# A graph layer on one core: where layernorm's transposition stands, who tests 37 of 50 rows, and how the last sum gets its operands

## The chip, the cores and the metric

The kernel runs on one core of one Trainium2 chip. Its time is the device time of one execution in microseconds; the number that counts is the median over the runs. One further execution was taken with the hardware profiler, and its trace is what the views below show.

The engines are called as in the profile: PE is TensorE (PEld its weight loads), DVE is VectorE, ACT is ScalarE, POOL is GpSimd, SP is SyncE, which only issues transfers here. Each engine works through its own instructions in order and waits where one of them needs something that another engine or a transfer has yet to finish.

## The reference

There are 6250 nodes with 128 channels (`x`) and 206,250 edges (`src`, `dst`), sorted by `dst`; a loop on each node is among them.

```python
h   = relu(layernorm(x))                      # per node, over the 128 channels
msg = concat(h[dst], h[src] - h[dst]) @ W.T + b
out = x + segment_max(msg, dst)               # maximum over the edges of each destination
```

As `W` has two halves, the message is `A[dst] + B[src]` with `A = h @ (W1 - W2).T + b` and `B = h @ W2.T`. `A` doesn't change within a segment. So `out = x + A + max over the edges of B[src]`.

## The kernel before, in words

Nodes are numbered `p * 49 + d`: partition `p` of 128 owns 49 destinations (`LD`), and its edges stand in a window of 1792 (`WIN`). Sources are numbered `q * 125 + l` (50 blocks `q`, 125 rows `l`). Most edges of a window are handled by one-hot matrices on PE; the rest, at most 440 to a partition after balancing (`KL`), are fetched row by row. The schedule is by hand: the order in which the Python code issues instructions is the order on each engine's queue (transfers on SP, ACT and POOL included).

**First stage (up to about 192 us).** `dst` and `src` windows are gathered. L736 turns `dst` into a float relative to the partition (`dlf`, on ACT), L740 makes `dl` of it, DVE makes `q16` of `src`, and then come 45 tests (`shift`, `deep`, `off`): DVE compares the keys with a shifted copy (`eq`, three buffers), PE adds the results in PSUM (`count`, `dup`). From this follow the edges that are alone in their cell and those that remain; `bases` (with a small product on PE, L606, whose result is `rowbase`), eleven `move`s and `spread` pack the remaining ones, POOL scatters them to `rest_list` in DRAM (L618, two scatters), and SP loads the balanced list from there (`qa<-rest_list`, L634). From that load DVE makes `ridx` (L808), the row numbers for the gathers.

Beside this runs layernorm with the products for A and B, in 30 calls of `step()`: six before the tests, three among them, three after them, and the rest in one go, all before `move` in the code. Call `i` works on five pairs of blocks at once. Before the change its order is:

```python
piece(i - 5, 1); piece(i - 4, 0); keep_all(i - 4); store(i - 4)  # ACT, and SP's stores of A and B
relu(i - 2)                                                      # ACT: pt -> hT
norm(i, 0); norm(i, 1)                                           # ACT: x -> xn
turn(i - 1)                                                      # PE: two transpositions xn -> pt
weigh(i - 3, 0); weigh(i - 3, 1)                                 # PE: hT times weights, and the bias
less(i - 4, 0)                                                   # PE: takes the rounded part of B away
```

In the profile `turn` is L667, `relu` L671, `weigh` L677 and L679, `less` L691, `piece` L687, `keep_all` L684, `norm` L662. `pt` is one tile with two halves. The stores go through SP's queue, ahead of the load of `rest_list`.

**Main loop (about 192 to 787 us).** There are 13 tiles of ten `l` values (the last of eight), 490 columns each, and 25 pairs of blocks to a tile: 325 turns `k`. In each, PE makes two products `z`, ACT turns them into one-hot columns (`oh`, L858), PE multiplies these with B in two pieces (`ps`, four matmuls, L943), and DVE takes the maximum (L947). Beside it the next tile is prepared: of the 50 rows of `OHQ`, row `a` up to `SQ` comes from ACT as a sign of `2 q - 2 a + 1` (`sgn`, L236, one instruction each), the others from DVE by comparison (`is_q`, L239), and PE takes the differences of neighbouring sign rows out again with the matrix `Diff`. DVE also makes `OHD` (L243, L246), and PE multiplies the two (L285).

The rest of the edges runs as a chain of rows: `gather_row` has POOL issue an indirect load of one row of B for each partition (L105, 440 of them), `stream_step` has DVE fold it into the row before (L188, `G`), and every eight rows SP writes them to `M`. A gather may be at most 16 rows ahead of the chain (`LEAD`). Gathers carry eight semaphores in turn, so each waits for the one eight before it. About 1.45 rows belong to a turn of the loop, 1.6 in the first tile. The chain is over at the first turn of the last tile, which the code calls `fixed` (`k` = 300).

**Last stage.** SP copies the last row to the next partition (`tail`, L956), DVE mends the heads with it, POOL scatters these to `M` (L960), and then POOL gathers the last row of each destination from `M` (`extract`, 49 gathers at L105), four at a time from `k` = 303 on. Meanwhile the last tile's turns run. At the end PE transposes the dense maxima, DVE takes the maximum with the extracted rows (L1002) and adds `xa` (L1007), and the result is stored in groups of eight. `xa` is A + x: at the first turn of the last tile SP loads A into it (L925), and at turn 15 of that tile POOL issues a load of `x` that adds to what is there (L899).

Of the kernel before, what the change touches and what calls it, by code (L numbers as in the profile page):

```python
# [31 lines left out]
F32 = mybir.dt.float32  # L32
# [6 lines left out]
AF = mybir.ActivationFunctionType  # L39
# [19 lines left out]
U = 8  # L59
# [1 line left out]
LEAD = 16  # L61
TL = 10
NEAR = 4
SQ = 25


def divisor_near(n, target, most):
# [3 lines left out]
def gnn_kernel(tc, x, src, dst, W, b, out):  # L71
# [42 lines left out]
    with ExitStack() as ctx:  # L114
# [13 lines left out]
        with ExitStack() as body:  # L128
# [81 lines left out]
            def onehots(t):  # L210

                if t >= len(tiles):
                    return [], []
                l0, nl = tiles[t]
                h = hots[t % 2]
                if t < 2:
                    oneh[t] = (h.tile([P, NBLK, Q + 1, TL], BF16, name="OHQ"),
                               h.tile([P, NBLK, WD, TL], BF16, name="OHD"))  # L220
                    G_.memset(oneh[t][0][:, :, 0], 1.0)
                else:
                    oneh[t] = oneh[t - 2]
                oq, od = oneh[t]
                ls = slice(l0, l0 + nl)

                def each(ap, b0, b1, n):

                    return at(ap, b0 * P + l0, [list(ap.ap[0]), [P, b1 - b0], [0, n], [1, nl]])

                def every(ap, b0, b1, n):

                    return at(ap, 0, [list(ap.ap[0]), [0, b1 - b0], [TL, n], [1, nl]])

                def sgn(a):
                    A_.activation(oq[:, :, a, :nl], TQ[:, :, ls], AF.Sign, scale=2.0, bias=sbias[:, a:a + 1])  # L236

                def is_q(b0, b1):
                    V.tensor_tensor(oq[:, b0:b1, SQ + 1:, :nl], each(TQ, b0, b1, Q - SQ), every(qq, b0, b1, Q - SQ),  # L239
                                    ALU.is_equal)  # L240

                def is_d():
                    V.tensor_tensor(od[:, :, :, :nl], each(TD, 0, NBLK, WD), every(jj, 0, NBLK, WD), ALU.is_equal)  # L243

                def val_of():
                    V.tensor_tensor(od[:, :, :, :nl], od[:, :, :, :nl], each(TV, 0, NBLK, WD), ALU.mult)  # L246

                def val_last():
                    def all_(ap):
                        return ap.rearrange("p (o b) -> p o b", o=1).to_broadcast([P, LD, NBLK])  # L250

                    od_last = oneh["last"] = accp.tile([P, LD, NBLK], BF16, name="od_last")
                    tdl = accp.tile([P, NBLK], BF16, name="tdl")
                    V.tensor_tensor(tdl, TD[:, :, P - 1], lob, ALU.subtract)
                    V.tensor_tensor(od_last, all_(tdl), dd.to_broadcast([P, LD, NBLK]), ALU.is_equal)
                    V.tensor_tensor(od_last, od_last, all_(TV[:, :, P - 1]), ALU.mult)

                half = NBLK // 2
                return [lambda a=a: sgn(a) for a in range(1, SQ + 1)], \
                       [lambda: is_q(0, half), lambda: is_q(half, NBLK), is_d, val_of] + \  # L260
                       [val_last] * (t == len(tiles) - 1)

            def products(t, bank):
# [42 lines left out]
            with ExitStack() as pre:  # L306
# [358 lines left out]
                def turn(i):  # L665
                    for j in range(2):
                        T_.transpose(st["pt", i][:, j, :L], st["xn", i][:, j], ident[:L, :L])  # L667
# [21 lines left out]
                def less(i, e):  # L689

                    T_.matmul(st["pm", i][:L, :, :C], negid[:L, :L], Bp[:L, e, 2 * i:2 * i + 2], start=False,  # L691
                              stop=True, skip_group_check=True)
# [11 lines left out]
                def step():  # L704


                    i = made["ln"]
                    made["ln"] = i + 1

                    def on(d):  # L710
                        return 0 <= i - d < NH

                    if on(5):
                        piece(i - 5, 1)
                    if on(4):
                        piece(i - 4, 0)
                        keep_all(i - 4)
                        store(i - 4)
                    if on(2):
                        relu(i - 2)  # L720
                    if on(0):
                        norm(i, 0)
                        norm(i, 1)
                    if on(1):
                        turn(i - 1)
                    if on(3):
                        weigh(i - 3, 0)
                        weigh(i - 3, 1)
                    if on(4):
                        less(i - 4, 0)  # L730

                STEPS = NH + 5
                for _ in range(6):
                    step()

                A_.activation(dlf, dwin, AF.Relu, bias=nthr)  # L736
                V.tensor_scalar(qa, swin, -62.0, 0.008, op0=ALU.add, op1=ALU.mult)
                V.tensor_scalar_add(qa, qa, MAGIC)
                V.tensor_scalar_add(q16, qa, -MAGIC)
# [15 lines left out]
                for n, f in enumerate(tests):  # L755
                    f()
                    if n == 6:
                        A_.activation(mids, mids, AF.Square)
                    if n % 14 == 8:
                        step()  # L760
                    elif n % 5 == 2 and early:
                        turned(*early.pop(0))
                    if n >= 20 and n % 5 == 0:
                        for g in signs[n - 20:n - 15]:
                            g()
                    if n in (12, 24, 36):
                        moments(3 + n // 12)
                        averages(3 + n // 12)
                        scales_a(3 + n // 12)
                    if n in (14, 26, 38):  # L770
                        scales_b(3 + n // 12)
                assert not early
                for g in signs[25:]:
                    g()
                cmp_.close()
                late = pre.enter_context(tc.tile_pool(name="late", bufs=1, side="right", reuse_waits="tile"))
                first = late.tile([P, W2], BF16, name="first")
# [25 lines left out]
                V.scalar_tensor_tensor(val, dlf, float(-L), first, op0=ALU.add, op1=ALU.mult)  # L803
                for b0 in range(0, NBLK, 4):
                    turned(val, TV, b0)
                for f in vals[:3]:
                    f()
                V.tensor_scalar(ridx, parts[:, 1:], 8191, None, op0=ALU.bitwise_and)  # L808
                vals[3]()
                bank0 = ps_m.tile([P, 512], F32, name="pm")  # L810
                mats, rest = products(0, lambda: bank0)
                for f in mats + rest:
# [26 lines left out]
            with ExitStack() as main:  # L839
# [51 lines left out]

                    return [flags, flagged] + [lambda a=a: find(a) for a in range(0, n8, 8)] + [rows_of_m]

                def add_x():

                    for p0, p1, g, n in ((0, P - 16, LD, 4), (P - 16, P - 1, LD, 4), (P - 1, P, LASTD, 2)):
                        m = g * C // n
                        assert m * n == g * C and m <= 2048
                        G_.dma_start(at(xa, 0, [[xa.ap[0][0], P], [m, n], [1, m]])[p0:p1],  # L899
                                     at(x, p0 * LD * C, [[LD * C, p1 - p0], [m, n], [1, m]]), accum_op=ALU.add, max_dma_last_dim=4 * m)  # L900

                oh = z_and_onehot(*pairs[0])
                soon, hot_fs = list(onehots(1)), [[], []]
# [2 lines left out]
                def due(k):  # L906

                    return min(NS, int(1.6 * min(k, NP_) + 1.45 * max(k - NP_, 0)))

                xa = None  # L910
                acc2 = None
                fixed, extracted, headed = 0, 0, False
                lasts = last_rows()
                for k, (t, i) in enumerate(pairs):
                    n = cols[t]
                    left = NP_ - i // 2
                    if i == 0:
                        acc2 = two.tile([P, 2, 512], F32, name="acc2")
                        if t == len(tiles) - 1:
                            hotx.close()  # L920
                            fin = main.enter_context(tc.tile_pool(name="fin", bufs=3, side="right",
                                                                  reuse_waits="tile"))
                            xa = fin.tile([P, LD, C], F32, name="xa", bufs=1)
                            for p0, p1, d0, g in ((0, P - 16, 0, LD), (P - 16, P - 1, 0, LD), (P - 1, P, 0, LASTD)):
                                nc.sync.dma_start(xa[p0:p1, d0:d0 + g], at(At, p0 * LD * C, [[LD * C, p1 - p0], [1, g * C]]))  # L925

                            nc.sync.dma_start(xa[P - 1:P, LASTD:], at(At, 0, [[LD * C, 1], [1, (LD - LASTD) * C]]))
                        new_products = products(t + 1, lambda: ps_v.tile([P, 512], F32, name="pv"))
                        mats, rest = new_products or ([], [])
                        if t:  # L930
                            hot_fs = list(onehots(t + 2))
# [31 lines left out]
                    elif fixed and k > fixed + 2 and k % 2:  # L963
# [2 lines left out]
                            if d == extracted:  # L966
                                follow(g, maxed)
                        extracted = min(extracted + 4, LD)
                    if xa is not None and i == 30:
                        add_x()  # L970
                    some(soon[0], 10 - i // 2)
                    some(soon[1], 8 - i // 2)
                    some(hot_fs[0], left - 5)
# [7 lines left out]
                                          for j in range(2)), ALU.max)  # L981
                    if k % 6 == 0 and k > 2 * NP_ and lasts:
                        lasts.pop(0)()
                assert state["ran"] == NS and fixed + 2 < len(pairs)
                for d in range(extracted, LD):
                    extract(d)
                mid.close()
# [5 lines left out]
                acc_v = acc.rearrange("c (p d) -> c d p", d=LD)  # L993
                for d0 in range(0, LD, U):
                    g = min(U, LD - d0)
                    o = fin.tile([P, U, C], F32, name="o", bufs=3)
                    for j0 in range(0, g, 4):
                        j1 = min(j0 + 4, g)
                        pf = ps_f.tile([P, 4, P], F32, name="pf")
# [77 lines left out]
```

## Time and profile before

| | |
|---|---|
| median of 3 runs | 888.58 us (886.48 to 889.82) |
| profiled execution, own time | 884.34 us |
| its span | 882.5 us |
| busy PE, DVE | 707.6 us, 707.5 us (80% each) |
| busy ACT, POOL | 527.8 us, 524.6 us (60%, 59%) |
| first gather of B's rows starts | 192.35 us |
| last one starts | 772.23 us |
| first and last extraction gather start | 797.00 us, 871.65 us |

Busy shares are means over the three stages, which have different limits; each stage has to be read by itself. In a row of the timeline the first number is the start in us, the second the time until the last of the merged instructions ended; behind the shapes stands in brackets how long the engine had been idle, and who ended that. In the waits, the numbers are total us, times and the longest. A group's row gives busy us, mean ns of one, and the idle time ahead of them with what ended it.

### The profile page before, as it was taken

To read this page: it belongs to the slowest core of one execution; us is meant where nothing else is said; L and a number is where in the kernel's file an instruction comes from. 1 tells how busy PE (TensorE), PEld (TensorE's weight loads), DVE (VectorE), ACT (ScalarE), POOL (GpSimd) and SP (SyncE) were. 2 spreads that over 40 slices of the span, in tenths; PEclk is the share of its full clock that TensorE was granted. 3 is DMA by queue.
4 is the path that set the end of the run, shared out by engine and by line. 5 is a ranking of instruction groups with operands and counts; after the bars stand their busy time and mean duration, and the time that the engine had idled before them with its cause. 6 is when DMAs were issued, how large, how long until landed. Compare 5 with 4: busy or idle time off the path is not lost. (4 is left out here: it accounts for less than half of the span.)

```text
span 882.5 us, 13139 instructions
## 1 busy us (share of the span) xinstructions
PE 707.6 (80%) x4275; PEld 501.4 (57%) x4275; DVE 707.5 (80%) x1177; ACT 527.8 (60%) x1224; POOL 524.6 (59%) x582
## 2 busy tenths in 40 slices
PE   1478776767999999999999999999898989849310
PEld 0234343454767776767676666667666767538210
DVE  6499779537899999999998889989898998737223
ACT  0424644437787878787778677777777776626000
POOL 4500000127777777777777777777777777707734
PEclk9999855557999999999999999999999999968655
DMA  6550022221454333333333333333333333451384
GB/s 155 148 117 24 24 64 53 59 78 48 150 194 141 123 97 123 100 99 96 99 97 113 103 103 99 100 100 98 99 96 101 103 112 108 140 138 47 76 184 135
DMA packets 48467, 91.39 MB, mean 104 GB/s; under 512 B 10964, under 2 KB 30395, under 8 KB 48036
## 3 DMA queue, kind: packets, MB, share of 16 engines
q0 software_dynamic: 17264, 40.98, 18.6%
q1 hardware_dynamic: 30120, 49.04, 16.6%
q10 hardware_dynamic: 1009, 0.49, 0.3%
q8 instruction: 34, 0.56, 0.3%
q14 instruction: 40, 0.33, 0.1%
HBM read 45.64 MB, written 44.71 MB: 102 GB/s over the span
## 5 line engine op out<-in xcount | busy, mean ns | idle before, releaser
L105 POOL DMA_INDIRECT G<-Bt,ridx x440 | 445.6, 1013 | 163.8 <-issue 88.1
L858 ACT ACTIVATE oh<-z 126x490 fp32r<-126x490 f32 (+1 forms) x650 | 335.5, 572 | 165.7 <-PE z L857 164.3
L943 PE MATMUL ps<-oh,Bp 126*128 126x490 f32 (+1 forms) x1300 | 395.6, 427 | 36.4 <-DVE acc L947 31.0
L947 DVE TENSOR_TENSOR acc<-acc,ps 128x980 f32<-128x980 f32 (+1 forms) x312 | 360.0, 1154 | 12.6 <-PE ps L943 10.4
L943 PEld LDWEIGHTS ps<-oh,Bp 126*128 126x128 f32 x1300 | 242.3, 195 | 126.3 <-DVE acc L947 70.0
L857 PE MATMUL z<-Vf,Sel 114*126 114x490 f16 (+1 forms) x650 | 198.1, 384 | 10.1 <-ACT oh L858 7.9
L188 DVE SCALAR_TENSOR_TENSOR G<-G,slim 128x128 f32<-128x128 f32 x439 | 152.9, 348 | 48.6 <-DMA G<-Bt,ridx 43.0
L236 ACT ACTIVATE OHQ<-TQ,sbias 128x140 bf16<-128x140 bf16 (+1 forms) x325 | 122.7, 413 | 0.5
L285 PEld LDWEIGHTS <-OHQ 128*51 128x51 bf16 x1792 | 92.1, 184 | 39.7 <-issue 39.7
L857 PEld LDWEIGHTS <-Sel 114*126 114x126 f16 x650 | 81.9, 139 | 30.6 <-issue 3.6
L285 PE MATMUL pv<-OHD,OHQ 128*51 128x13 bf16 (+5 forms) x1638 | 94.9, 240 | 0.5 <-ACT OHQ L236 0.5
L618 POOL DMA_INDIRECT rest_list<-qa,base_i x2 | 3.4, 1706 | 110.4 <-DVE qa L627 108.2
L105 POOL DMA_INDIRECT G<-M,last_e x48 | 45.5, 948 | 27.6 <-issue 14.5
L667 PE MATMUL pt<-ident,xn 125*128 125x125 f32 x50 | 16.1, 419 | 41.9 <-ACT hT L671 32.4
L554 PE MATMUL dup<-eq,identb 128*128 128x512 bf16 (+1 forms) x180 | 40.7, 361 | 9.3 <-DVE eq L559 7.9
L687 ACT CAST Bp<-pm 125x256 fp32r<-125x256 f32 x50 | 16.2, 374 | 50.8 <-PE pm L691 48.6
L677 PE MATMUL pm<-wT,hT 128*125 128x256 f32 x100 | 43.3, 582 | 0.0
L1001 PE MATMUL pf<-ident,acc 128*128 128x128 f32 x49 | 10.6, 391 | 34.5 <-DVE o L1002 32.8
L667 PEld LDWEIGHTS pt<-ident,xn 125*128 125x128 f32 x50 | 7.0, 193 | 49.5 <-ACT hT L671 39.3
L554 PEld LDWEIGHTS <-identb 128*128 128x128 bf16 x180 | 17.5, 99 | 29.2 <-issue 14.5
L1007 DVE TENSOR_TENSOR o<-o,xa 128x1024 f32<-128x1024 f32 (+1 forms) x7 | 7.7, 1093 | 31.4 <-DMA xa<-in_x 31.2
L677 PEld LDWEIGHTS pm<-wT,hT 128*125 128x125 f32 x100 | 27.5, 303 | 4.0
(236 smaller groups left out, 472.5 us busy)
## 6 DMA issues: line engine op xcount, KB each, us to landing
M<-G SPq DMA_DIRECT2D x63, 512.0 KB
G<-Bt,ridx POOLq DMA_INDIRECT x440, 2.6
xa<-At SPq DMA_DIRECT2D x1, 2744.0 KB
xa<-in_x POOLq DMA_DIRECT2D x1, 2744.0 KB
G<-in_x SPq DMA_DIRECT2D x6, 448.0 KB
Bt<-ba SPq DMA_DIRECT2D x12, 224.0 KB
At<-ba SPq DMA_DIRECT2D x12, 224.0 KB
out_x<-o SPq DMA_DIRECT2D x3, 512.0 KB
```

Of the source, the lines that this page charges most:

```text
L105: return G_.indirect_dma_start(out=o, out_offset=None, in_=table, in_offset=bass.IndirectOffsetOnAxis(ap=idx, axis=0))
L188: steps.append(V.scalar_tensor_tensor(G[:, j], state["prev"], slim[:, k:k + 1], G[:, j], op0=ALU.min, op1=ALU.max))
L236: A_.activation(oq[:, :, a, :nl], TQ[:, :, ls], AF.Sign, scale=2.0, bias=sbias[:, a:a + 1])
L285: T_.matmul(o, oq[:, b_, :, l], r, start=k == 0 and b_ == 0, stop=b_ == NBLK - 1, skip_group_check=True)
L554: T_.matmul(dup[:, c0:c1], identb, e[:, c0:c1], start=s == 1, stop=s == SH + 2)
L667: T_.transpose(st["pt", i][:, j, :L], st["xn", i][:, j], ident[:L, :L])
L677: T_.matmul(pm[:L, j], st["hT", i][:, j, :L], wT, start=j == 0, stop=False, skip_group_check=True)
L687: A_.copy(Bp[:L, e, 2 * i:2 * i + 2], st["pm", i][:L, :, :C])
L857: T_.matmul(z[:, :n], Sel[:, i + j], Vf[t % 2][:, :n], start=True, stop=True)
L858: A_.activation(oh[:, j, :n], z[:, :n], AF.Relu)
L943: T_.matmul(ps[:, j, :n], Bp[:, e, i + j], oh[:, j, :n], start=e == 0, stop=e == 1)
L947: maxed = V.tensor_tensor(acc2[:, :, :n], acc2[:, :, :n], ps[:, :, :n], ALU.max)
```

## The change

Four things are changed.

- `turn(i - 1)` moves from the middle of `step()` to its end, behind `weigh` and `less`.
- `SQ` goes from 25 to 37: ACT makes 37 rows of `OHQ` by signs, and DVE compares 13 (before 25). DVE's comparison comes as one instruction instead of two. The first tile's signs are spread over the tests in groups of three.
- The conversion of `dst` goes from ACT to DVE.
- `xa` is filled differently. A and x come in four pieces of 13, 13, 13 and 10 destinations to a partition, both loaded by SP (x into a tile `xo` of its own with two buffers), at the 3rd, 7th, 11th and 15th turn after `fixed`; DVE adds the first two pieces at the 11th and 15th turn, the others between the groups of output. POOL's adding load is gone. The output tile `o` has two buffers instead of three.

```diff
-SQ = 25
+SQ = 37
...
-                return ... [lambda: is_q(0, half), lambda: is_q(half, NBLK), is_d, val_of] + \
+                return ... [lambda: is_q(0, NBLK), is_d, val_of] + \
...
                     if on(0):
                         norm(i, 0)
                         norm(i, 1)
-                    if on(1):
-                        turn(i - 1)
                     if on(3):
                         weigh(i - 3, 0)
                         weigh(i - 3, 1)
                     if on(4):
                         less(i - 4, 0)
+                    if on(1):
+                        turn(i - 1)
...
-                A_.activation(dlf, dwin, AF.Relu, bias=nthr)
+                V.tensor_scalar(dlf, dwin, nthr, 0.0, op0=ALU.add, op1=ALU.max)
...
-                    if n >= 20 and n % 5 == 0:
-                        for g in signs[n - 20:n - 15]:
-                            g()
+                    if n >= 18 and n % 2 == 0:
+                        for g in signs[:3]:
+                            signs.pop(0)()
...
-                def add_x():
-                    for p0, p1, g, n in ((0, P - 16, LD, 4), (P - 16, P - 1, LD, 4), (P - 1, P, LASTD, 2)):
-                        ...
-                        G_.dma_start(<xa[p0:p1]>, <x>, accum_op=ALU.add, max_dma_last_dim=4 * m)
+                def load_some():
+                    d0 = adds[-1][1] if adds else 0
+                    d1 = min(d0 + XG, LD)                    # XG = 13
+                    xo = fin.tile([P, XG, C], F32, name="xo", bufs=2)
+                    for o, ap in ((xa[:, d0:d1], At), (xo[:, :d1 - d0], x)):
+                        ...                                  # nc.sync.dma_start for 112, 15 and 1 partitions
+                    adds.append((d0, d1, xo))
+                def add_some(n):
+                    d0, d1, xo = adds[n]
+                    V.tensor_add(xa[:, d0:d1], xa[:, d0:d1], xo[:, :d1 - d0])
...
                             xa = fin.tile([P, LD, C], F32, name="xa", bufs=1)
-                            for p0, p1, d0, g in ...:
-                                nc.sync.dma_start(xa[p0:p1, d0:d0 + g], <At>)
...
-                    if xa is not None and i == 30:
-                        add_x()
+                    if fixed and k - fixed in (11, 15):
+                        add_some((k - fixed) // 4 - 2)
+                    if fixed and k - fixed in (3, 7, 11, 15):
+                        load_some()
...
                 for d0 in range(0, LD, U):
-                    o = fin.tile([P, U, C], F32, name="o", bufs=3)
+                    if d0 in (16, 32):
+                        add_some(1 + d0 // 16)
+                    o = fin.tile([P, U, C], F32, name="o", bufs=2)
```

More of the change, by code (lines that the diff above doesn't have):

```diff
@@ L256, in val_last @@
                     V.tensor_tensor(od_last, od_last, all_(TV[:, :, P - 1]), ALU.mult)
-                half = NBLK // 2
                 return [lambda a=a: sgn(a) for a in range(1, SQ + 1)], \
-                       [lambda: is_q(0, half), lambda: is_q(half, NBLK), is_d, val_of] + \
+                       [lambda: is_q(0, NBLK), is_d, val_of] + \
                        [val_last] * (t == len(tiles) - 1)
@@ L771, in gnn_kernel @@
                         scales_b(3 + n // 12)
-                assert not early
-                for g in signs[25:]:
-                    g()
+                assert not early and not signs
                 cmp_.close()
@@ L805, in gnn_kernel @@
                     turned(val, TV, b0)
-                for f in vals[:3]:
+                for f in vals[:2]:
                     f()
                 V.tensor_scalar(ridx, parts[:, 1:], 8191, None, op0=ALU.bitwise_and)
-                vals[3]()
+                vals[2]()
                 bank0 = ps_m.tile([P, 512], F32, name="pm")
@@ L892, in last_rows @@
                     return [flags, flagged] + [lambda a=a: find(a) for a in range(0, n8, 8)] + [rows_of_m]
-                def add_x():
-                    for p0, p1, g, n in ((0, P - 16, LD, 4), (P - 16, P - 1, LD, 4), (P - 1, P, LASTD, 2)):
[L897 to L900, printed above, removed]
+                def load_some():
[3 more added lines that the diff above has]
+                    for o, ap in ((xa[:, d0:d1], At), (xo[:, :d1 - d0], x)):
+                        for p0, p1, g in ((0, P - 16, d1), (P - 16, P - 1, d1), (P - 1, P, min(d1, LASTD))):
+                            if g > d0:
+                                nc.sync.dma_start(o[p0:p1, :g - d0],
+                                                  at(ap, (p0 * LD + d0) * C, [[LD * C, p1 - p0], [1, (g - d0) * C]]))
+                        g = max(d0, LASTD)
+                        if d1 > g:
+                            nc.sync.dma_start(o[P - 1:P, g - d0:], at(ap, 0, [[LD * C, 1], [1, (d1 - g) * C]]))
+                    adds.append((d0, d1, xo))
+                def add_some(n):
+                    d0, d1, xo = adds[n]
+                    V.tensor_add(xa[:, d0:d1], xa[:, d0:d1], xo[:, :d1 - d0])
                 oh = z_and_onehot(*pairs[0])
@@ L908, in due @@
                     return min(NS, int(1.6 * min(k, NP_) + 1.45 * max(k - NP_, 0)))
+                XG = 13
+                adds = []
                 xa = None
@@ L923, in gnn_kernel @@
                             xa = fin.tile([P, LD, C], F32, name="xa", bufs=1)
-                            for p0, p1, d0, g in ((0, P - 16, 0, LD), (P - 16, P - 1, 0, LD), (P - 1, P, 0, LASTD)):
-                                nc.sync.dma_start(xa[p0:p1, d0:d0 + g], at(At, p0 * LD * C, [[LD * C, p1 - p0], [1, g * C]]))
-                            nc.sync.dma_start(xa[P - 1:P, LASTD:], at(At, 0, [[LD * C, 1], [1, (LD - LASTD) * C]]))
                         new_products = products(t + 1, lambda: ps_v.tile([P, 512], F32, name="pv"))
@@ L983, in gnn_kernel @@
                         lasts.pop(0)()
-                assert state["ran"] == NS and fixed + 2 < len(pairs)
+                assert state["ran"] == NS and tiles[-1][0] == pairs[fixed][0] * TL and adds[-1][1] == LD
                 for d in range(extracted, LD):
```

## The prediction

> **What bounds the kernel now.** I read the page first, then windows over the stages, the waits, the timeline of one layernorm step, and the timeline of the last hundred microseconds. Three stages have three different limits.
>
> The windows, columns being busy us of PE, PEld, DVE, ACT, POOL, then granted clock, DMA share and GB/s:
>
> ```profile
> 100.00:130.00 30.00, 18.58 (x50) 11.24 (x50) 22.64 (x23) 15.60 (x42) 0.00 (x0) 0.57 0.20 51
> 130.00:160.00 30.00, 20.73 (x52) 12.50 (x53) 29.10 (x33) 13.92 (x39) 1.35 (x2) 0.50 0.22 60
> 160.00:192.00 32.00, 21.25 (x65) 12.99 (x64) 7.00 (x7) 13.85 (x37) 2.06 (x1) 0.55 0.30 80
> ...
> 495.00:542.00 47.00, 43.79 (x277) 30.91 (x277) 42.02 (x66) 34.31 (x77) 36.03 (x37) 1.00 0.33 105
> ```
>
> From 100 to 192 us no engine is full and PE has half its clock: a chain is running. The waits say which:
>
> ```profile
> DVE o L1007 <- DMA xa<-in_x: 31.2, 1, 31.2
> ...
> POOL G L105 <- DVE ridx L808: 30.3, 1, 30.3
> DVE ridx L808 <- DMA qa<-rest_list: 25.0, 1, 25.0
> ...
> DVE dl L740 <- ACT dwin L736: 11.0, 1, 11.0
> ```
>
> The first gather (192.35) waits for `ridx`, that for the load of `rest_list`, and this load stands on SP behind every layernorm store, though its scatters were issued by 162. So layernorm's pace ends last. One step takes 4.80 us (130.19 to the next `turn` at 135.00), in single file:
>
> ```profile
> 129.73 0.41 ACT L671 ACTIVATE hT<-pt 128x250 f32<-128x250 f32 x1
> ...
> 130.19 0.68 PE L667 MATMUL pt<-ident,xn 125*128 125x125 f32 x2 [1.51 <-ACT hT L671]
> ...
> 130.66 1.92 PE L677 MATMUL pm<-wT,hT 128*125 128x256 f32 x4
> ...
> 132.51 0.47 PE L679 MATMUL pm<-b,onesb 3*125 3x256 bf16 x1
> ...
> 132.91 0.58 PE L691 MATMUL pm<-Bp,negid 125*125 125x256 f32 x1
> ...
> 133.52 0.65 ACT L687 CAST Bp<-pm 125x256 fp32r<-125x256 f32 x2 [2.64 <-PE pm L691]
> ```
>
> PE's `turn` stands first in its queue and waits for ACT's `relu`; ACT stands still for 2.64 us until `less` ends.
>
> In the main loop the page's costliest group tells it:
>
> ```profile
> L105 POOL DMA_INDIRECT G<-Bt,ridx x440 | 445.6, 1013 | 163.8 <-issue 88.1
> ```
>
> Without the 30.3 us ahead of the first, 133.5 us of idle lie before 439 gathers: 0.304 us each, an issue gap. POOL never waits longer, so it sets the pace: 1.013 + 0.304 = 1.317 us a row, 36.25 rows a tile, 47.7 us; the tiles take 47. DVE, PE and ACT have slack.
>
> At the end:
>
> ```profile
> 766.52 1.49 SPq L925 DMA_DIRECT2D xa<-At  x3
> ...
> 771.80 0.35 DVE L188 SCALAR_TENSOR_TENSOR G<-G,slim 128x128 f32<-128x128 f32 x1 [2.97 <-DMA G<-Bt,ridx]
> ...
> 777.10 0.35 DVE L188 SCALAR_TENSOR_TENSOR G<-G,slim 128x128 f32<-128x128 f32 x1 [3.86 <-DMA G<-Bt,ridx]
> ...
> 840.38 0.94 POOL L105 DMA_INDIRECT G<-M,last_e  x1 [0.30 <-issue]
> 850.91 0.94 POOL L105 DMA_INDIRECT G<-M,last_e  x1 [9.59 <-DMA xa<-in_x]
> ```
>
> The 3.1 MB load of `xa` starves the last six gathers, so the chain of rows ends at 786.6 though the last was issued at 772.2; later POOL's own adding load blocks its extraction gathers.
>
> **The change part by part**, in time of the profiled execution: span 882.5, own time 884.34, which is 4.24 under the median of 888.58.
>
> *DVE converts dst.* DVE idled 10.97 us before L740 (41.57). The conversion costs it about 1.2 us (L737, the same size from int32: 1.218), and its tests could start at 36 instead of 45.7. PE comes later: it must finish six layernorm steps, 42.46 before. With `turn` last in them I work them to 39.7 (each `weigh` starts one ACT relay earlier). Three `eq` buffers let DVE run ahead, then its fourth test waits for the first count, 1.3 us at slow clock: 41.0 against 48.69. Gain 7.7 us.
>
> *`turn` last.* New order on PE: `weigh` 1.85, bias 0.40, `less` 0.42, `turn` 0.47, the start-to-start times above: 3.14 us. ACT's `pieces`, `keep_all`, `relu`, `norm` take 2.2 us (133.52 to 135.7) and now run during `weigh`. So a step costs 3.14 at the slow clock. At full clock (91.09 to 92.8) PE needs 1.70, and ACT's 2.2 would be the limit. First use: L606 came after three such steps, `rowbase` at 114.53; now DVE's own `heads` (109.15 - 7.7 = 101.5) ends last and `rowbase` comes at 102.3: 12.2 earlier. DVE then runs unbroken to the scatters (156.39 and 159.95 become 144.2 and 147.8), landed by about 152, as the second waited 3.56 for the first. Second use: fourteen whole steps from 102.2 end at 133 (2.2) or 146 (3.14), the four lighter ones and stores add 6 to 10: SP is free at 139 to 156. What is late next is therefore the scatters or, at slow clock, the stores. `rest_list` takes 2.58 (188.61 to 191.19): `ridx` at 154.6 to 158.3 instead of 191.19. I take 156: **35 us gained**. The clock rows weigh both ways: 0.50 to 0.57 in this stage with PE 62 to 69% busy, 1.00 in the main loop at 93%; the new step would be full. [...]
>
> *37 rows by signs.* DVE's two `is_q` of 1.067 become one of about 1.10 (L243, the same 1820 elements): 1.03 us less per tile, which DVE's slack hides. It touches POOL, though: at 501.01 a gather took 1.74 where `is_q` began at 500.86, 1.76 at 509.38 beside `is_d`. 35 of the 440 gathers took over 1.1 us, 19.9 us in excess of 0.95; four such DVE operations per tile become three, so a quarter goes: **5 us gained** (0 to 9). ACT gets twelve signs more per tile at 0.30 to 0.415: 3.6 to 5.0 us on 34.3 of 47; covered. (The first tile's fall among the tests, where ACT is busy 16.65 of 30 us.) If the cover went, see the third rival. In the first tile four signs stand beside a pair instead of three (1.2 + 0.92 = 2.1 us a pair against the 2.1 of 1.6 rows): 0 to 3 us; I take 0, because POOL is then up to 16 rows ahead.
>
> *Load of xa moved.* It now stands on SP behind the last `M<-G` and `tail<-G`, so the last gathers land undisturbed: a gather landed 2.42 after its start in the chain (812.02), then two DVE rows of 0.3: the chain of rows ends 3.0 after the last gather instead of 14.4: **11.4 gained**.
>
> *From the end of the rows to the end.* Before: 10.4 until the first extraction (`tail` 6.3, `head`, scatter), 74.65 from the first to the 49th, 10.85 to the end; 95.9. Now the three loads on POOL (3.2 us), their 11.9 of waits and more leave: 48 x 1.245 = 59.8. Against it stand 6.27 MB of loads beside the gathers, some 26 us at 240 GB/s (3.74 MB in 15.5 us from 766.5). Under such a load a gather landed only every 2.85 us (771.80 to 785.89, five intervals). With eight in flight (each waits for the one eight before) I count 16 issued where 18.5 would have been: 3 us lost, and 1.6 on `head`'s scatter. Bounds: nothing, or 20 if everything waits until the loads are through. 12.0 + 59.8 + 3 + 10.85 = 85.7: **10.2 gained**. DVE's four adds of 1664 elements cost 2.0 each (1.227 per 1024), and two stand between the last tile's pairs: a late piece stalls PE there, but these pairs need 27 us and POOL 60, so it is hidden. Fewer `o` buffers: groups come every 10 us, hidden. [...]
>
> Sum: 35 + 5 + 11.4 + 10.2 = 61.6. Own time 884.3 - 61.6 = 822.7; on the runs' median 888.6 - 61.6 = **827**.
>
> **Rivals.**
> 1. Layernorm's relay stays: `turn` and `relu` still take turns at 4.8 us. Then only the 7.7 of the conversion is gained in front, 34.3 in all: 854. For it: ACT's `relu` still waits for `turn`. Against: `weigh`, the longest piece, no longer stands behind that.
> 2. The loads choke the extraction: `head`'s scatter waits for the first two pieces, and gathers land at 2.85 throughout, 15 to 20 instead of 4.6 us: 840. For it: the rows at 771 to 786. Against: pieces three and four wait for DVE's adds.
> 3. Slower: ACT becomes the main loop's bound. It decides where a pair's chain, `z` 0.58, relus 1.05 and two signs 0.82, runs in series: 2.45 against 1.88 us in 17 pairs of 12 tiles, 116 us: 943. From 2.18 us a pair on it eats the whole gain. Against: the first tile has three signs a pair already, and its relus start at 212.35, 214.17, 216.00, 1.83 apart.
>
> **How the numbers follow.** Forecast 0.68, first rival 0.12, second 0.14, third 0.06. Range: the good ends together (clock 1.4, signs 4, no contention 4.6, and profiles against medians up to 4) give 813, a little below it 808; the bad ends (layernorm 2.3, signs 5 and 3, tail 15) give 852, with the first rival 855. Faster by over 0.5% (4.4 us, about what a measurement can tell from no change): 0.93; within: 0.01; slower: 0.06.
>
> **What would show it.** First gather at 156 to 160; a `turn` every 2.2 to 3.2 us; gather mean near 1.00 us with gaps still 0.30; no wait of DVE `G` for its gather over 1 us at the end; the first extraction 12 us after the last row, POOL unbroken afterwards. A wait of POOL on DVE in the main loop, or of ACT's `relu` as long as 2.6 us, would make it wrong.

## The result, and the profile after

| | before | after |
|---|---|---|
| median | 888.27 us (886.48 to 889.82, 4 runs) | 828.64 us (827.97 to 830.31, 4 runs) |
| profiled execution, own time | 884.34 us | 829.12 us |
| its span | 882.5 us | 827.4 us |

The ratio is 0.9332, with an interval of 0.9309 to 0.9355: 59.6 us are gained on the medians. The forecast was 827. Between the two profiled executions only 55.1 us lie, because the profiled run of before was 3.9 under its median and that of after 0.5 above its own. The prediction's sum was 61.6, made against the profile. So the forecast came closer than its sum did, and the sum is what has to be examined.

**First stage.** The first lines are from the timeline of after (start, duration, engine, line; idle time ahead in brackets): two successive layernorm steps, from one `turn` (L666) to the next.

```profile
111.36 0.43 PE L666 MATMUL pt<-ident,xn 125*128 125x125 f32 x2
111.62 1.03 PE L676 MATMUL pm<-wT,hT 128*125 128x256 f32 x4
...
112.58 0.32 PE L678 MATMUL pm<-b,onesb 3*125 3x256 bf16 x1
...
112.90 0.46 ACT L670 ACTIVATE hT<-pt 128x250 f32<-128x250 f32 x1
113.13 0.38 PE L690 MATMUL pm<-Bp,negid 125*125 125x256 f32 x1 [0.23 <-ACT ba L683]
...
113.42 0.43 PE L666 MATMUL pt<-ident,xn 125*128 125x125 f32 x2
```

A step takes 2.06 us instead of 4.80. PE goes from `turn` straight into `weigh`, and `relu` starts when PE's bias product ends and runs beside `less`. The window over 90 to 136 us (busy us of PE, PEld, DVE, ACT, POOL, then granted clock, DMA share, GB/s), of before and then of after:

```profile
90.00:136.00 46.00, 32.20 (x112) 18.87 (x112) 36.92 (x41) 24.28 (x66) 0.00 (x0) 0.66 0.17 45
```
```profile
90.00:136.00 46.00, 38.25 (x157) 23.99 (x154) 41.74 (x35) 40.73 (x113) 0.00 (x0) 0.93 0.43 112
```

PE issues 157 instead of 112 instructions and gets a clock of 0.93 instead of 0.66; `weigh` falls from 582 to 435 ns. ACT, busy 40.73 of 46, now sets the step: PE waits 0.23 us for it ahead of each `less` (DVE's 41.74 are the packing). How much of the shorter step is the order itself and how much the clock is not shown, as no run holds the clock down. Behind that, the timeline shows what ends last:

```profile
135.67 0.83 SPq L698 DMA_DIRECT2D At<-ba  x2
...
143.00 1.30 POOL L617 DMA_INDIRECT rest_list<-qa,base_i  x1 [91.69 <-DVE qa L626]
...
146.56 2.10 POOL L617 DMA_INDIRECT rest_list<-qa,base_i  x1 [2.26 <-DVE first L798]
150.28 0.35 SPq L633 DMA_DIRECT2D qa<-rest_list  x1
152.78 0.39 DVE L805 TENSOR_SCALAR ridx<-qa 128x440 int32<-128x440 int32 x1 [0.90 <-DMA qa<-rest_list]
153.95 1.12 POOL L105 DMA_INDIRECT G<-Bt,ridx  x1 [5.29 <-DVE ridx L805]
```

SP issues its last layernorm store at 135.67, before the scatters. These now end last, and `ridx` waits 0.90 us for its load instead of 25.0.

**Main loop.** The page's group and the waits:

```profile
L105 POOL DMA_INDIRECT G<-Bt,ridx x440 | 443.0, 1007 | 138.9 <-issue 89.3
```
```profile
POOL G L105 <- issue: 102.4, 337, 0.3
```

A gather takes 1007 instead of 1013 ns, with the same 0.30 us behind it. The first to the last gather take 577.36 us (153.95 to 731.31) against 579.88.

**The end.** From the timeline:

```profile
733.93 0.35 DVE L188 SCALAR_TENSOR_TENSOR G<-G,slim 128x128 f32<-128x128 f32 x1 [0.35 <-DMA G<-Bt,ridx]
...
735.59 3.10 SPq L899 DMA_DIRECT2D xa<-At  x3
...
742.18 1.00 POOL L967 DMA_INDIRECT M<-head,head_i  x1 [9.93 <-DVE head L966]
...
751.80 0.97 POOL L105 DMA_INDIRECT G<-M,last_e  x1 [8.62 <-DVE acc L954]
...
753.60 1.89 DVE L909 TENSOR_TENSOR xa<-xa,xo 128x1664 f32<-128x1664 f32 x1
...
754.34 1.96 POOL L105 DMA_INDIRECT G<-M,last_e  x1 [0.30 <-issue]
```

The chain of rows ends at 734.28, 3.0 after the last gather. But the first extraction starts 9.62 us after `head`'s scatter, where before it started 3.00 after it:

```profile
794.00 1.00 POOL L960 DMA_INDIRECT M<-head,head_i  x1 [20.83 <-DVE head L959]
797.00 0.97 POOL L105 DMA_INDIRECT G<-M,last_e  x1 [2.00 <-issue]
```

The wait is put down to a maximum of DVE; the first extraction follows the one of its own turn, which had long been done, so the scatter's landing was the suspect. A second thing to see is the gather of 1.96 us beside DVE's add.

### The profile page after: what moved, and what is told of

It reads as the page before. It is cut to its first block, busy times and chain, and to the rows that moved or that the text cites. A ratio compares the mean times of both kernels' runs of the same rounds, so it can differ in the third digit from the quotient of the medians.

```text
span 827.4 us, 13330 instructions
## 1 busy us (share of the span) xinstructions
PE 678.8 (82%) x4270; PEld 488.1 (59%) x4275; DVE 704.5 (85%) x1169; ACT 566.7 (68%) x1379; POOL 523.5 (63%) x579
## 4 chain that ended last, share of the span: by engine, by line
DVE 24%; PE 23%; DMA 19%; issue 14%; ACT 11%; POOL 8%; SPq 1%; POOLq 0%; ACTq 0%; DVEq 0%
DMA G<-Bt,ridx 13%; PE ps L950 10%; DVE acc L954 9%; POOL G L105 8%; PE z L854 5%; ACT oh L855 5%; PE pv L284 4%; ACT OHQ L236 3%; DVE G L188 3%; DVE dwin L598 3%; DVE eq L558 2%; DVE qa L597 1%; PE dup L553 1%; DMA w_sb<-in_L_gnn_W 1%; DMA xo<-in_x 1%
## 5 line engine op out<-in xcount | busy, mean ns | idle before, releaser
L105 POOL DMA_INDIRECT G<-Bt,ridx x440 | 443.0, 1007 | 138.9 <-issue 89.3
L236 ACT ACTIVATE OHQ<-TQ,sbias 128x140 bf16<-128x140 bf16 (+1 forms) x481 | 170.1, 414 | 0.5
L105 POOL DMA_INDIRECT G<-M,last_e x48 | 50.2, 1046 | 22.9 <-issue 13.1
L1013 DVE TENSOR_TENSOR o<-G,pf 128x512 f32<-128x512 f32 x12 | 8.1, 685 | 29.5 <-DMA G<-M,last_e 28.3
L553 PEld LDWEIGHTS <-identb 128*128 128x128 bf16 x180 | 17.7, 99 | 25.8 <-issue 11.4
L676 PE MATMUL pm<-wT,hT 128*125 128x256 f32 x100 | 30.6, 435 | 0.3 <-DVE rowbase L606 0.3
L558 DVE TENSOR_TENSOR eq<-KA,KB 128x1792 bf16<-128x1792 int16 x22 | 23.9, 1088 | 0.8 <-PE dup L553 0.8
L1012 PEld LDWEIGHTS pf<-ident,acc 128*128 128x128 f32 x49 | 8.7, 220 | 26.0 <-DVE o L1013 24.1
L558 DVE TENSOR_TENSOR eq<-KA 128x1792 bf16<-128x1792 int16 x21 | 22.8, 1084 | 1.4 <-PE dup L553 1.4
L661 ACT ACTIVATE xn<-G,nmr,rstd 125x128 f32<-125x128 f32 x48 | 22.3, 549 | 0.0
```

What stands on the lines that cost most here:

```text
L105: return G_.indirect_dma_start(out=o, out_offset=None, in_=table, in_offset=bass.IndirectOffsetOnAxis(ap=idx, axis=0))
L553: T_.matmul(dup[:, c0:c1], identb, e[:, c0:c1], start=s == 1, stop=s == SH + 2)
L558: V.tensor_tensor(e, KA[:, 64:], i1, ALU.is_equal)
L676: T_.matmul(pm[:L, j], st["hT", i][:, j, :L], wT, start=j == 0, stop=False, skip_group_check=True)
```

## The experiments

Theory: four terms stand side by side, layernorm's step (largest), dst's conversion, the undisturbed last gathers, and the end, where the first pieces of A and x delay `head`'s scatter. Rivals: the relay of PE and ACT was not the cause of the first term; the wait before the extraction is one for DVE's pairs; PE, DVE or ACT set the main loop's pace and not POOL.

### Each part alone, on the kernel before

The first takes the new order of the step and nothing else:

```diff
-                    if on(1):
-                        turn(i - 1)
                     if on(3): ...
                     if on(4): ...
+                    if on(1):
+                        turn(i - 1)
```

> The kernel before with one edit: layernorm's transposition (turn) moved to the end of its step. My theory (layernorm's relay between PE and ACT sets the time up to the first gather): a turn every 2.0 to 2.4 us instead of 4.80, the wait for rest_list gone, the first gather at 157 to 163 instead of 192.35 (dst's conversion stays on ACT, so DVE's tests start some 5 us later than in the changed kernel, at most 8), so 30 to 34 us gained: 854 to 858 by the median of 888. If the relay stays (my first rival), the step remains at 4.8 and no more than 3 us is gained: 885 or more.

Measured: 850.4 us, ratio 0.9599 (0.9567 to 0.9632), by which it is 35.6 us less; that is better than the 854 to 858 that were expected. A `turn` comes every 2.06 us (115.27, 117.33, 119.39). The scatters start at 147.50 and 151.06, and DVE no longer stands idle for the load behind them; the first gather waits for `ridx`:

```profile
157.26 0.39 DVE L808 TENSOR_SCALAR ridx<-qa 128x440 int32<-128x440 int32 x1
...
158.43 1.12 POOL L105 DMA_INDIRECT G<-Bt,ridx  x1 [5.27 <-DVE ridx L808]
```

The second takes the conversion alone:

```diff
-                A_.activation(dlf, dwin, AF.Relu, bias=nthr)
+                V.tensor_scalar(dlf, dwin, nthr, 0.0, op0=ALU.add, op1=ALU.max)
```

> The kernel before with one edit: VectorE converts dst (dlf) instead of ScalarE. My theory: DVE's fourth test comes at 42.5 to 44.5 instead of 48.69 (PE's six steps in the old order end at 42.46), rowbase some 5 earlier; but the layernorm stores still stand ahead of rest_list's load, so the first gather comes only as much earlier as PE's steps do: 0 to 5 us gained, 883 to 888. Rival: the stores were not what ended last, and all 7.7 us of my sum come out: 880.

Measured: 882.04 us, ratio 0.9935 (0.991 to 0.996), 3.6 to 8.0 us less; in its trace the first gather comes at 189.22, 3.1 earlier. A step still takes 4.80 us:

```profile
111.70 0.68 PE L667 MATMUL pt<-ident,xn 125*128 125x125 f32 x2 [1.29 <-ACT hT L671]
116.50 0.68 PE L667 MATMUL pt<-ident,xn 125*128 125x125 f32 x2 [1.51 <-ACT hT L671]
```

and `ridx` still waits 25.9 us for `rest_list`. The time alone doesn't decide between the theory and the rival, as 3.6 to 8.0 includes the rival's 7.7; the wait for `rest_list` and the 3.1 us do. (In the kernel with the pieces alone, below, whose first stage is that of before, the first gather comes at 194.32, so one profile against another can be 2 us off.) As long as layernorm ends last, part of DVE's head start is hidden. Beside the new order it seems to come out: the first gather comes 4.48 earlier in the changed kernel (153.95) than with the order alone (158.43), though these two differ by more than the conversion.

The third takes the signs alone:

```diff
-SQ = 25
+SQ = 37
...
-                       [lambda: is_q(0, half), lambda: is_q(half, NBLK), is_d, val_of] + \
+                       [lambda: is_q(0, NBLK), is_d, val_of] + \
...
```

> The kernel before with one edit: 37 instead of 25 of the one-hot rows by ScalarE's signs, one is_q instead of two, the first tile's signs spread. My theory (each such VectorE operation lengthens one gather on POOL, which sets the pace): 2.5 us gained, since the changed kernel's gathers ran 2.5 shorter than before; 5 was predicted; 883 to 888. Rival (ScalarE becomes the bound of the main loop): slower by over 5.

Measured: 886.43 us, ratio 0.9998 (0.9981 to 1.0014): between 1.7 us less and 1.2 more, so no difference that can be told. First to last gather take 578.49, 1.4 less than before. I set the gathers of over 1.1 us, of before and of this kernel, against what DVE did beside them. Before, 12 stood beside an `is_q` alone (24 of these instructions), 6.7 us over 0.95 in sum, and 14 beside `is_d` or `val_of` of full size, 8.1 us. Here 7 stand beside `is_q` (12 instructions), 4.9 us, and 16 beside the two others, 10.4 us. The instructions that were left met more gathers. The sum over all long gathers is 20.3 against 19.9. It also changes where the signs don't: with the order alone, and 25 signs, it is 16.0, and the first to the last gather take 577.44.

The fourth takes the pieces alone:

```diff
-                            for p0, p1, d0, g in ...: nc.sync.dma_start(xa..., At...)   # whole, with the last rows
-                    if xa is not None and i == 30:
-                        add_x()
+                    if fixed and k - fixed in (11, 15):
+                        add_some((k - fixed) // 4 - 2)
+                    if fixed and k - fixed in (3, 7, 11, 15):
+                        load_some()
...
```

> The kernel before with one edit: A and x come in four pieces after the last row and are added by VectorE. My theory: the chain of rows ends 3.0 after the last gather instead of 14.4, so 11.4 gained; the end after it is 2.8 shorter as in the changed kernel: 14 gained, 874. Rival (the loads' cost at the end was due to the other parts): with the 10.2 of my sum for that part, 21.6 gained, 867.

Measured: 872.27 us, ratio 0.9835 (0.9811 to 0.986), 14.7 less. The rows end 2.9 after the last gather, and the wait of the changed kernel is there again:

```profile
786.06 1.00 POOL L970 DMA_INDIRECT M<-head,head_i  x1 [10.26 <-DVE head L969]
...
795.11 0.97 POOL L105 DMA_INDIRECT G<-M,last_e  x1 [8.05 <-DVE acc L957]
```

The four gains by their ratios, 35.6, 5.8, 0.2 and 14.7, add up to 56.3 of 59.3 (what 0.9332 is of 888.27), within what the intervals allow.

### Four kernels on another chip

These ran together on a chip on which the kernel before took 1057.23 us (1048.32 to 1062.39, 11 runs), so their times say nothing on the terms. The first is the changed kernel with the first load held back:

```diff
-                                nc.sync.dma_start(o[p0:p1, ...
+                                l = nc.sync.dma_start(o[p0:p1, ...
+                                if not adds and p0 == 0 and ap is At:
+                                    follow(l, mended[0])
...
-                        G_.indirect_dma_start(out=M[:, :], ...
+                        mended[0] = G_.indirect_dma_start(out=M[:, :], ...
```

> The changed kernel with one wait added: the first piece of A and x is loaded only when the scatter of head has landed. My theory (the scatter and the load of tail share the DMA engines with the first two pieces, which costs 7 us on the way to the first extraction): the first extraction comes 10.4 us after the last row instead of 17.5, as before; the pieces then fall on the first extractions, which gives back 0 to 4: 3 to 7 us gained against the changed kernel, 822 to 826. Rival: the bytes have to be moved at some time, and what the scatter gains the extraction loses: 828 to 830.

The second leaves the loads and the adds out, so that its output lacks x and A:

```diff
-                        add_some(...)
-                        load_some()
...
-                    V.tensor_add(o[:, :g], o[:, :g], xa[:, d0:d0 + g])
+                    V.tensor_add(o[:, :g], o[:, :g], o[:, :g])
```

> The changed kernel without the loads of A and x and without their adds (the output adds the maximum to itself instead, so it leaves x and A out). My theory: what the loads cost beside the extraction goes. The first extraction comes 10.4 us after the last row instead of 17.5, and the 48 intervals after it take 48 x 1.245 = 59.8 instead of 64.8: 12 us less than the changed kernel, 816. If the wait until the first extraction is one for VectorE's pairs (as the trace labels it) and not for the loads, only the 5 go: 823.

The third goes on with the signs:

```diff
-SQ = 37
+SQ = 49
...
-                            for g in signs[:3]:
+                            for g in signs[:4]:
```

> The changed kernel with 49 instead of 37 rows by signs (four at a time in the first tile). If each VectorE operation for the one-hot lengthens a gather, the smaller is_q gives up to 2.5 us; ScalarE's busy time per tile of 47 us goes from 39 to about 44: my third rival (ScalarE in the pair's chain) would show as some pairs over 1.88 us and a wait of POOL on VectorE over 1 us: 5 us or more slower. My theory: within 3 us of the changed kernel, 826 to 832.

The fourth loads POOL with more gathers:

```diff
                 g = gather(Gt[i][:, j], Bt[:, :], ridx[:, k:k + 1])
+                if k >= 48 and k % 12 == 0:
+                    gather(spare[k // 12 % 2], Bt[:, :], ridx[:, k:k + 1])
```

> The changed kernel with 33 gathers more: from row 48 on, every twelfth row is gathered a second time into a spare tile that nothing reads. If POOL sets the main loop's pace (my theory): 33 x 1.31 = 43 us more, 872. If PE, VectorE or the pairs of ScalarE set it and POOL is merely asked at that pace, nothing or less than 10 us more.

Measured, in that order: 1016.53, 1018.47, 1022.09 and 1074.01 us. In the first three POOL did not set the main loop's pace. With the held load it waits 200.3 us for DVE's folding of the rows (187.4 and 173.0 in the next two), and 48% of the chain that ended last are PE's:

```profile
POOL G L105 <- DVE G L188: 200.3, 93, 6.5
```

The window over 400 to 500 us of this kernel, and then of the changed kernel in its first profile:

```profile
400.00:500.00 100.00, 79.52 (x456) 58.28 (x454) 71.88 (x118) 63.70 (x150) 58.49 (x60) 0.86 0.24 78
```
```profile
400.00:500.00 100.00, 95.36 (x633) 69.64 (x631) 88.68 (x140) 82.88 (x196) 77.02 (x76) 1.00 0.32 98
```

What can be read is the wait before the extraction: 10.28 us after the last row with the held load and 10.43 without loads, against 16.93 in the kernel with 49 signs, which has the loads where the change puts them. It is the loads and not DVE's pairs. The fourth kernel doesn't fit its expectation: where POOL doesn't set the pace it should have taken less than 10 us more, and it took 52 to 57 more than the other three, with its own runs between 1054 and 1079, though POOL waits 197.1 us for DVE in it as well. Why stays open. Whether the whole gains by the held load, whether POOL sets the pace, and what 49 signs cost could not be told here; the signs were not tried again.

### Three of them again, beside the changed kernel

On a chip like the first (before: 887.31 us):

> The changed kernel once more, on the same chip as its neighbours, for comparison: 828.6, if the chip is like the first; first extraction 17.5 after the last row, extraction 64.8.

Measured: 828.12 us, ratio 0.9325 (0.9306 to 0.9344); first extraction 16.70 after the last row, the 48 intervals after it 65.50.

> The changed kernel with one wait added, as in e5: the first piece of A and x is loaded only when the scatter of head has landed. On a chip where the kernel before takes 888: the first extraction 10.7 us after the last row instead of 17.5 (e5 showed 10.66 on the other chip), and after it POOL sends its gathers 1.25 apart whatever the loads do, so 5 to 7 us gained against the changed kernel, 821.5 to 824. Rival (what the scatter gains, the extraction loses): the extraction takes 70 instead of 64.8, 828 to 830.

Measured: 821.8 us, ratio 0.9258 (0.9239 to 0.9276), 6.3 less than its neighbour. The scatter lands in the time that it took before the change:

```profile
742.07 1.00 POOL L970 DMA_INDIRECT M<-head,head_i  x1 [9.27 <-DVE head L968]
744.50 1.12 SPq L899 DMA_DIRECT2D xa<-At  x3
745.07 0.97 POOL L105 DMA_INDIRECT G<-M,last_e  x1 [2.00 <-issue]
```

The first extraction comes 10.32 after the last row (10.28 on the other chip, and not the 10.66 of the expectation), and the 48 intervals take 65.36: the rival, that the extraction would give it back, falls. This version beats both kernels.

> The changed kernel without the loads of A and x and without their adds, as in e8 (the output leaves x and A out), on a chip where the kernel before takes 888. First extraction 10.7 us after the last row. My reading of the trace (the extraction's 4.6 us over 48 x 1.26 are gathers of 1.2 to 2.0 us beside VectorE's adds, not beside the loads): 60 to 61 for the extraction, 11 to 12 us gained, 817. If they come from something else, the extraction stays at 64.8 and only 7 go: 822.

Measured: 818.11 us, ratio 0.9227 (0.9198 to 0.9257), 10.0 less than the changed kernel; the extraction starts 10.30 after the last row and its 48 intervals take 61.87. The gathers, in the page of the changed kernel's first profile and then of this one:

```profile
L105 POOL DMA_INDIRECT G<-M,last_e x48 | 50.2, 1046 | 22.9 <-issue 13.1
```
```profile
L105 POOL DMA_INDIRECT G<-M,last_e x48 | 47.2, 984 | 16.3 <-issue 13.9
```

Beyond the first wait (8.62 and 2.00) POOL idles 14.3 us in both, 0.30 for each gather, so no gather of the extraction waits for a transfer, loads or no loads. The 3 us between them are in the gathers' own durations: in the changed kernel eight take 1.1 to 2.0 us, all beside DVE's adds (754.34 above), and the gathers that fall beside the loads without an add take 0.94 to 0.97. Here four take 1.3 to 1.7, three of them beside the adds of the output.

> The changed kernel with 33 gathers more into a spare tile, as in e9, on a chip where the kernel before takes 888. If POOL sets the main loop's pace: 33 x 1.31 = 43 us more, 872, with POOL's gaps still 0.30. If PE, VectorE and ScalarE, busy 36 to 44 of 47 us a tile, are what POOL follows: less than 10 more.

Measured: 864.55 us, ratio 0.9751 (0.9725 to 0.9777), 36.4 more than its neighbour; 43 were expected. From its page:

```profile
L105 POOL DMA_INDIRECT G<-Bt,ridx x440 | 438.0, 995 | 138.8 <-issue 86.5
...
L105 POOL DMA_INDIRECT spare<-Bt,ridx x33 | 31.6, 958 | 10.1 <-DMA G<-Bt,ridx 5.8
```

The 33 gathers cost POOL 31.6 us and 10.1 of gaps, 41.7, and the gaps of the others stay 0.30. The rows' own gathers fall from 1008 (its neighbour's page) to 995 ns, which is 5.7 us for 440: 20 of them take over 1.1 us, against 32 in the kernel without loads. 41.7 less 5.7 is 36.0. So on this chip POOL sets the pace of the main loop, though PE, DVE and ACT are busy 38.7 to 44.4 of 47 us in a tile of the changed kernel.

## Why the prediction was right, and where it was not

**Bounds and order.** The three stages were read rightly: layernorm's relay ended last in front (the order alone gives 35.6 us), POOL sets the pace in the middle (33 more gathers cost 36.4 us), and the time of the loads decided the end of the rows (the pieces alone end them 2.9 after the last gather).

**dst on DVE.** Said: fourth test at 41.0. It starts at 40.53, after a wait of 1.45 for the count. `rowbase` was said for 102.3; it comes at 101.02.

**`turn` last.** Said: a step of 3.14 us if the clock stays low, or 2.2 bound by ACT if it opens, and `ridx` between 154.6 and 158.3. The clock opened (0.93 granted over 90 to 136 us, 0.66 before) and the step is 2.06. The scatters end last, as the text expected for that case. They came at 143.00 and 146.56 (said 144.2 and 147.8), and `ridx` at 152.78, 3.2 before the 156 that was taken and 1.8 before the bound. Of the 3.2, 1.4 are the value chosen between the two clocks, 1.2 the scatters, and 0.6 the way from the second scatter to `ridx`, which took 6.2 and not 6.8. The first gather thus came 38.4 earlier instead of 35. The 0.93 was granted with PE busy 38.25 of 46 us and waiting 0.23 us at a time, the 0.66 of before with 32.20 of 46 and waits of 1.51; what opened the clock, no run shows.

**37 rows by signs.** Said: 5 us, a quarter of the long gathers' excess; the bound was 0 to 9. The excess stayed, 19.9 and 20.1 us. The stretch of gathers shrank by 2.5 in the changed kernel and by 1.4 with the signs alone, and the time of that kernel didn't change. With the order alone and 25 signs the stretch shrank by 2.4 as well, so the 2.5 are not shown to come from the signs. The step that failed is "four such DVE operations per tile become three, so a quarter goes": it took the loss as a fixed price per instruction. The rows show that it depends on which gather an instruction meets, and the remaining ones met more. Why they did was not tried. ACT's cover held: no wait of POOL on DVE in the main loop is of the size of the third rival.

**The last gathers.** Said: rows end 3.0 after the last gather, 11.4 gained. Measured: 2.97 and 11.4.

**From the rows' end to the end.** Said 85.7, measured 93.1: this is the largest miss, 7.4 us. The first extraction was said for 12.0 after the rows and came at 17.5. The step that failed is "1.6 on `head`'s scatter". Of what it is over 10.4, 0.5 is `tail`'s load (a wait of 5.31 against 4.79) and 6.6 the scatter's landing, 9.62 against 3.00; with the load held back 3.00 is there again. This was the first half of the second rival, that the scatter waits for the first pieces. The extraction was said to take 62.8 and took 64.82 (65.50 when the kernel ran again). Its extra was put down to late landings, at 2.85 us apiece under load; that reason is wrong, as no gather of the extraction waited for a transfer, and without loads and adds 2.95 are saved, all in the gathers' own durations. The price of 2.85 (the rows at 771.80 to 785.89 give 2.82) came from rows that DVE had to fold one after the other; in the extraction POOL goes on without waiting for a gather to land.

**The sum.** By the steps 38.4 + 2.5 + 11.4 + 2.8 = 55.1, which is the difference of the spans; said were 35 + 5 + 11.4 + 10.2 = 61.6. The 2.5 stand for the gathers, whatever shortened them. Of the 6.5 too many, 4.4 were made good by chance, since the profiled run of before was 3.9 under its median and that of after 0.5 above its own. Other profiles of unchanged stages hint at where the 3.9 lie: with the pieces alone the first gather comes 2.0 later than in the profile of before, and with the conversion alone the rows end 15.7 after the last gather, where 14.4 was taken.

**The rivals.** The relay did not stay (a step of 2.06 us with the order alone). The loads delayed the scatter, but not the gathers. ACT did not become the bound.

## What to carry to other kernels

Where two engines relay through one tile, order the queue so that the longest piece stands in front of the instruction that waits for the partner, and look for what ends last next before pricing the rest; here a step fell from 4.80 to 2.06 us, with a granted clock of 0.93 instead of 0.66. A large load that is moved off one chain has to be looked for on the next: here a short transfer on the critical path took three times as long beside it (9.62 us to the gather behind it, against 3.00), and one wait that held the load back for 9 us gave 6.3 us. A loss that a few instructions show beside another engine's work is not a price per instruction; fewer of them need not mean less of it: here the excess was 19.9 us before and 20.1 after.

## What the runs showed of the hardware

- POOL issued the extraction's gathers with gaps of 0.30 us all through the loads (DMA share 0.84, 214 GB/s from 733 to 770). The long ones, eight of 1.1 to 2.0 us, all stood beside DVE's f32 adds of two SBUF operands: one that began at 754.34 beside an add that ran to 755.49 took 1.96 us instead of 0.94. Without the loads and the adds of A and x the mean is 984 instead of 1046 ns.
- A scatter of 64 KB was followed by its dependent gather after 3.00 us alone and after 9.62 beside the first pieces of A and x (9.05 with the pieces alone, 8.92 with 49 signs, 8.50 in the changed kernel's second run, 8.44 with the 33 gathers more). Among the extraction's gathers none made POOL wait.
- The kernel before took 888.27, 887.29 and 887.31 us on three occasions and 1057.23 on another chip. There PE was granted 0.86 instead of 1.00 between 400 and 500 us (the kernel with the held load against the changed one), and it also stood still for reasons that the profile does not name, up to 8.0 us at a time:

```profile
PEld ps L952 <- issue: 153.4, 109, 8.0
```

That line is from the waits of the kernel with the held load on that chip. What was behind it stays open.
